# A four-block cross-attention kernel: in the last block all copies of transposed weights go to ScalarE, and half of the next step's exponentials are issued behind them

## The chip, the cores and the metric

The kernel runs on one core of a Trainium2 chip. The time is device time in microseconds (us) of one execution; the median of several runs counts. The engines of the core are TensorE (PE in the profile; PEld is its weight load), VectorE (DVE), ScalarE (ACT), GpSimd (POOL) and SyncE (SP, which issues most DMAs here).

## What is computed

Four blocks follow one another on `x` of shape (8, 112, 256), with a context of shape (8, 375, 192). Blocks 0 and 1 are self attention, cross attention and a gated MLP; block 2 is one cross attention; all of these have 16 heads of width 64. The last block has 16 heads of width 16, and is the one in which the change lies:

```python
h = _layernorm(x, ln1_w, ln1_b)
qkv = (h @ qkv_w + qkv_b).reshape(B, T, 3, H, HD)
q, k, v = [qkv[:, :, i].transpose(0, 2, 1, 3) for i in range(3)]
attn = jnp.einsum('bhtd,bhsd->bhts', q, k) * scale
attn = jnp.where(causal[None, None], neg, attn)
attn = jnp.where(tgt_mask[:, None, None, :], neg, attn)
attn = jax.nn.softmax(attn, axis=-1)
sa = jnp.einsum('bhts,bhsd->bhtd', attn, v).transpose(0, 2, 1, 3).reshape(B, T, C)
x = x + sa @ proj_w + proj_b
h = _layernorm(x, ln2_w, ln2_b)
...
attn = jnp.einsum('bhtd,bhsd->bhts', q, k) * scale
attn = jnp.where(enc_mask[:, None, None, :], neg, attn)
attn = jax.nn.softmax(attn, axis=-1)
ca = jnp.einsum('bhts,bhsd->bhtd', attn, v).transpose(0, 2, 1, 3).reshape(B, T, C)
x = x + ca @ out_w + out_b
h = _layernorm(x, ln3_w, ln3_b)
h = jax.nn.gelu(h @ mlp1_w + mlp1_b, approximate=False)
x = x + h @ mlp2_w + mlp2_b
```

Here q, k and v of the second attention come from `h` and the context. All is fp32.

## The kernel before, in words

**Stages and steps.** The work is cut into stages 0 to 9: stages 0 to 2 and 3 to 5 are blocks 0 and 1, stage 6 is block 2, stage 7 the causal self attention of the last block, stage 8 its cross attention, stage 9 its MLP. An attention stage is a list of steps. A step takes some heads of one batch: in stage 8 four heads against 375 context positions (four steps a batch, 32 in all), in stage 7 eight heads against 112 positions (two steps a batch, 16 in all). The causal steps of a batch stand among the steps of stage 6 or 8, as soon as their batch is ready. From the last step of stage 6 on, all steps have 16-wide heads; this stretch is called "the block" below.

**One step** (`add_step`) has three parts. `emit_s` makes the scores by matmuls (L943) into two PSUM tiles of the "s" pool, which has just two, and calls `softmax` for each block of heads. For 16-wide heads `softmax` issues, head by head, a DVE operation (L894) that subtracts the scores from the mask, writes the result to SBUF and gives its minimum, and an exponential on ACT (L898) with that minimum as bias, which also sums the row into `bsums`. For 64-wide heads it issues one DVE maximum (L905), exponentials (L911), a reciprocal (L917) and a POOL multiplication (L920). `emit_t` transposes the weights on PE (L962), one PSUM tile of the "mm" pool for each bank of 4 x 112 columns (three banks in a cross step, two in a causal step), and copies the tile to SBUF (`wT`) by `evac`. `emit_pv` multiplies with the values (L985) and evacuates the result to `oT`.

**The "mm" ring** has four PSUM tiles. All of PE's products but the scores take their tile from it, in turn; a product waits until the tile of four allocations ago has been copied away.

**`evac`** copies from PSUM to SBUF on ACT (L343, L345, L347) or DVE (L351, L353, L355). It keeps a running load for both, to which `busy` adds the work that isn't `evac`'s, and takes the engine that would be done first by this account.

**Order.** PE's order is written out by a planner (`Plan`). In the main loop, iteration i emits the scores of step i + 2, on odd i the PV parts of steps i - 1 and i, then the transposes of step i + 1, and between these fillers that are due: projections (L663, L685, L710), keys (L751 and L760), values (L826 and L835), output products (L629), normalized `x` transposed (L597, evacuated to `hT`), MLP products (L1233). An item states what it depends on, and after how many us of planned time it may follow. The other engines' queues are set by a scheduler at build time, except for what stands in `tc.keep_in_program_order`. Each engine works its queue in order.

**Normalization of 16-wide heads** comes once for each batch, after its last step: item ("R", st, b) takes the reciprocal of the sums on DVE (L1019) and has POOL broadcast it to `rb` (L1020), and item ("N", st, b) transposes `rb` on PE (L1026) and scales `oT` on DVE (L1028). "R" may follow 4.0 us of planned time after the scores of the batch's last step. An output product (L629, added to `x` at L633) then prepares the next normalization (DVE L566, L568, L570; POOL L572, L574, L576).

Of the kernel before, what the change touches and what calls it, by code (L numbers as in the profile page):

```python
# [11 lines left out]
AF = mybir.ActivationFunctionType  # L12
# [3 lines left out]
B, T, D = 8, 112, 256  # L16
S, DC = 375, 192
# [282 lines left out]
def kernel(ctx: ExitStack, tc: tile.TileContext, a: dict, out: bass.AP):  # L300
    nc = tc.nc
# [19 lines left out]
    plan = Plan(RINGS, ARENA, lambda k: 512 if k[0] == "v" else S if k[0] == "k" and k[1] in (1, 4, 6, 8) else 4 * T)  # L321
# [7 lines left out]
    SEG = [0, 0, 0, 1, 1, 1, 2, 2, 2, 2]  # L329
    load = {"act": 0.0, "dve": 0.0}  # L330

    def busy(eng, us):
        load[eng] = max(load[eng], plan.now) + us
# [537 lines left out]
    bsums, pairs = {}, {}  # L871

    def add_step(st, b, blocks, dh, nk, qs, ks, qap, kap, vtile, mask, opos, ochunk, last=False, pair=None):
# [3 lines left out]
        s = len(steps)  # L877
        nch = (nk + P - 1) // P
        dp = 64 if dh == 64 else 32
        heads = [h for blk in blocks for h in blk]  # L880
        cell = {}

        def softmax(blk, ps):
            ns = len(blk) // 2
            sv = ps[:, :, : ns * nk].rearrange("p b (s k) -> p b s k", k=nk)
            pr = ppool.tile([T, 2, ns, nk], F32, tag="pr", name="pr")
            nm = small.tile([T, 2, 4], F32, tag="nm", name="nm")
            if dh == 16:

                for n, h in enumerate(blk):
                    bk, sl = n % 2, n // 2
                    nc.vector.tensor_tensor_reduce(  # L894
                        pr[:, bk, sl, :], sv[:, bk, sl, :], mask(), -1.0, -0.01 * NEG, ALU.add, ALU.min,
                        nm[:, bk, sl : sl + 1],
                    )
                    nc.scalar.activation(  # L898
                        pr[:, bk, sl, :], pr[:, bk, sl, :], AF.Exp, bias=nm[:, bk, sl : sl + 1], scale=-1.0,
                        accum_out=bsums[(st, b)][:, h : h + 1],  # L900
                    )
                    busy("dve", 0.16 + 0.00104 * nk)
                    busy("act", 0.46 + 0.00084 * nk)
                return pr
            nc.vector.tensor_reduce(nm[:, :, :ns], sv, AX.X, ALU.max, negate=True)  # L905
            busy("dve", 0.16 + 0.00104 * 2 * ns * nk)
            sums = small.tile([T, 2, 4], F32, tag="sums", name="sums")
            rinv = small.tile([T, 2, 4], F32, tag="rinv", name="rinv")
            for n in range(len(blk)):
                bk, sl = n % 2, n // 2  # L910
                nc.scalar.activation(  # L911
                    pr[:, bk, sl, :], sv[:, bk, sl, :], AF.Exp, bias=nm[:, bk, sl : sl + 1],
                    accum_out=sums[:, bk, sl : sl + 1],
                )
                busy("act", 0.46 + 0.00084 * nk)
                if nch > 1:
                    nc.vector.reciprocal(rinv[:, bk, sl : sl + 1], sums[:, bk, sl : sl + 1])  # L917

                    tc.keep_in_program_order(
                        nc.gpsimd.tensor_scalar_mul(pr[:, bk, sl, :], pr[:, bk, sl, :], rinv[:, bk, sl : sl + 1])  # L920
                    )
                    busy("dve", 0.16)
            if nch == 1:
                nc.vector.reciprocal(rinv[:, :, :ns], sums[:, :, :ns])  # L924
                tc.keep_in_program_order(
                    nc.gpsimd.tensor_tensor(  # L926
                        pr, pr, rinv[:, :, :ns].unsqueeze(3).to_broadcast([T, 2, ns, nk]), ALU.mult
                    )
                )
                busy("dve", 0.16)  # L930
            return pr

        def emit_s():
            if dh == 16 and (st, b) not in bsums:
                bsums[(st, b)] = small.tile([T, H], F32, tag="bsums", name="bsums")
            tiles = [ps_s.tile([T, 2, 512], F32, tag="s", name="s") for _ in blocks]

            order = [(i, n) for i, blk in enumerate(blocks) for n in range(len(blk))]
            if dh == 16:
                order.sort(key=lambda e: (e[1] // 2, e[0]))  # L940
            for i, n in order:
                h = blocks[i][n]
                nc.tensor.matmul(  # L943
                    tiles[i][:, n % 2, (n // 2) * nk : (n // 2 + 1) * nk], lhsT=qap(h), rhs=kap(h),
                    start=True, stop=True,
                )
            for i, blk in enumerate(blocks):
                pr = softmax(blk, tiles[i])
                for n, h in enumerate(blk):
                    cell[h] = pr[:, n % 2, n // 2, :]  # L950


        if nch == 1:
# [4 lines left out]
        def emit_t(bank):  # L958
            pt = mm_tile()
            kl = min(P, nk - bank[0][1] * P)  # L960
            for i, (h, c) in enumerate(bank):
                nc.tensor.transpose(  # L962
                    pt[:kl, i * T : (i + 1) * T], cell[h][:, c * P : c * P + kl], ident[:T, :T]
                )
            wt = tpool.tile([P, 448], F32, tag="wT", name="wT")
            n = len(bank) * T
            evac(wt[:kl, :n], pt[:kl, :n], n)
            for i, (h, c) in enumerate(bank):
                cell[(h, c)] = wt[:kl, i * T : (i + 1) * T]

        def emit_pv():
# [18 lines left out]
            if pair is not None and not second:  # L990
# [11 lines left out]
        par = P // dp  # L1002
        plan.add(Item(("S", s), len(heads) / par * nk * 4 / 2400 + 0.19, emit_s, uses=uq + uk,
                      deps=[] if mask is None else [(("mask", b if nk == S else "self"), 3.0)]), False)
        for i, bank in enumerate(banks):
            plan.add(
                Item(("T", s, i), 0.1 * len(bank), lambda bank=bank: emit_t(bank), deps=[(("S", s), 0)]), False
            )
        plan.add(
            Item(("PV", s), 0.193 * nch * len(heads) / par + 0.25, emit_pv, uses=uv,  # L1010
                 deps=[(("T", s, i), 0) for i in range(len(banks))]), False
        )
        steps.append(len(banks))
        if last:

            def emit_norm():

                rs = small.tile([T, H], F32, tag="rsum", name="rsum")
                nc.vector.reciprocal(rs, bsums.pop((st, b)))  # L1019
                nc.gpsimd.tensor_copy(rb, rs.unsqueeze(2).to_broadcast([T, H, 16]))  # L1020

            def emit_scale():
                rf = rb.rearrange("p h d -> p (h d)")
                ps = mm_tile()
                for c in range(2):
                    nc.tensor.transpose(ps[:, c * T : (c + 1) * T], rf[:, c * P : (c + 1) * P], ident[:T, :T])  # L1026
                cols = slice(b * T, (b + 1) * T)
                nc.vector.tensor_tensor(  # L1028
                    oT[:, 0:2, cols], ps[:, : 2 * T].rearrange("p (c t) -> p c t", t=T), oT[:, 0:2, cols], ALU.mult
                )  # L1030
                busy("dve", 0.31)

            prev = [(k, 0) for k in norms[-1:]]
            norms.append(("N", st, b))
            plan.add(Item(("R", st, b), 0, emit_norm, s + 0.4, deps=[(("S", s), 4.0)] + prev, seg=SEG[st]))
            plan.add(
                Item(("N", st, b), 0.2, emit_scale, s + 0.9, deps=[(("R", st, b), 2.0), (("PV", s), 1.2)], seg=SEG[st])
            )
# [65 lines left out]
    def first_of(st, b):  # L1104
        return at[(st, b, 0)]
# [183 lines left out]
    st = 0  # L1289
# [79 lines left out]
    for seg in range(3):  # L1369
        lo, hi = cuts[seg], cuts[seg + 1]  # L1370

        for s in (lo, lo + 1):
            for k in plan.items[("S", s)].uses + plan.items[("PV", s)].uses:
                mk = plan.maker.get(k)
                if mk is None or plan.items[mk].done:
                    continue
                if plan.items[mk].begin is not None:
                    plan.require(mk)
                else:
                    plan.drain(mk)  # L1380
        for i in range(lo - 2, hi):
            plan.step = i
            left = plan.pace(i, seg)
            plan.close_jobs()
            if lo <= i + 2 < hi:
                plan.main(("S", i + 2))

            if lo <= i < hi and (i - lo) % 2 == 1:
                plan.main(("PV", i - 1))
                plan.main(("PV", i))  # L1390
            if lo <= i + 1 < hi:
                n = steps[i + 1]
                share = left / (n + 2)
                left -= plan.fill(2 * share)
                for k in range(n):
                    plan.main(("T", i + 1, k))
                    left -= plan.fill(min(left, share))
            plan.fill(left)
            plan.open_jobs(1 if i + 1 >= first_of(8, 0) else 2, i + 3.5, seg)
    plan.step = len(steps)  # L1400
# [37 lines left out]
```

## Time and profile before

| | |
|---|---|
| median of 3 runs | 1664.54 us (1663.47 to 1664.8) |
| the profiled execution | 1663.88 us, span 1662.1 us |
| PE busy in the span | 1632.3 us (98%) |
| DVE busy | 825.7 us (50%) |
| ACT busy | 769.4 us (46%) |
| POOL busy | 718.3 us (43%) |
| DMA | 39.51 MB, mean 24 GB/s |
| exponentials of 16-wide heads (L898), 256 | 124.7 us busy, mean 488 ns, and 50.1 us of ACT idle before them until DVE's L894 |
| copies to `wT` on ACT (L347), 289 | 151.1 us, mean 533 ns |
| copies to `wT` on DVE (L355), 191 | 115.0 us, mean 612 ns |

The span is the time from the first to the last instruction on the core; the run's time is a little more. A group's row in the profile gives busy time, mean duration, and the idle time of that engine just before the group with what ended it. In the order of time, durations of neighbouring instructions on one engine overlap a little; the distance from start to start is what an instruction costs in a full queue. A view of waits gives, for a waiting line and what released it, the total, the number of times, and the longest.

### The profile page before, as it was taken

To read this page: it belongs to the slowest core of one execution; us is meant where nothing else is said; L and a number is where in the kernel's file an instruction comes from. 1 tells how busy PE (TensorE), PEld (TensorE's weight loads), DVE (VectorE), ACT (ScalarE), POOL (GpSimd) and SP (SyncE) were. 2 spreads that over 40 slices of the span, in tenths; PEclk is the share of its full clock that TensorE was granted. 3 is DMA by queue.
4 is the path that set the end of the run, shared out by engine and by line. 5 is a ranking of instruction groups with operands and counts; after the bars stand their busy time and mean duration, and the time that the engine had idled before them with its cause. 6 is when DMAs were issued, how large, how long until landed. Compare 5 with 4: busy or idle time off the path is not lost.

```text
span 1662.1 us, 30117 instructions
## 1 busy us (share of the span) xinstructions
PE 1632.3 (98%) x11772; PEld 1141.7 (69%) x11772; DVE 825.7 (50%) x2193; ACT 769.4 (46%) x2420; POOL 718.3 (43%) x689
## 2 busy tenths in 40 slices
PE   9999999999999999999999999999999999998999
PEld 7777666666667878666666665666666666765568
DVE  3444454544532344545444552344455556787762
ACT  3554434444531445434444452234444555676662
POOL 1324455556632223355565570364564448322110
DMA  5012020000101011000000010100000000000000
GB/s 186 5 50 56 3 87 1 1 26 1 52 29 45 1 29 52 26 1 30 1 2 26 1 45 29 33 23 1 1 1 1 16 1 26 30 2 2 2 2 23
DMA packets 26566, 39.51 MB, mean 24 GB/s; under 512 B 1543, under 2 KB 21559, under 8 KB 26423
## 3 DMA queue, kind: packets, MB, share of 16 engines
q1 hardware_dynamic: 25495, 36.74, 7.0%
q8 instruction: 93, 1.52, 0.4%
q10 hardware_dynamic: 864, 0.79, 0.1%
q14 instruction: 50, 0.41, 0.1%
q0 software_dynamic: 64, 0.05, 0.0%
HBM read 35.88 MB, written 0.92 MB: 22 GB/s over the span
## 4 chain that ended last, share of the span: by engine, by line
PE 91%; DVE 4%; ACT 3%; issue 1%; POOL 1%; DMA 0%; ACTq 0%; POOLq 0%; DVEq 0%
PE mm L629 12%; PE mm L663 11%; PE s L943 10%; PE mm L985 10%; PE mm L962 9%; PE mm L751 8%; PE mm L785 7%; PE mm L1198 6%; PE mm L760 5%; PE mm L794 4%; PE mm L710 4%; PE mm L1233 2%; ACT pr L898 2%; DVE pr L894 1%; ACT pr L911 1%
## 5 line engine op out<-in xcount | busy, mean ns | idle before, releaser
L920 POOL TENSOR_SCALAR pr<-pr,rinv 112x375 f32<-112x375 f32 x384 | 467.7, 1235 | 338.3 <-DVE rinv L917 338.1
L911 ACT ACTIVATE pr<-s,nm 112x375 f32<-112x375 f32 (+1 forms) x640 | 303.0, 491 | 168.4 <-DVE nm L905 166.2
L355 DVE COPY arena<-mm 128x375 f32<-128x375 f32 (+4 forms) x187 | 111.8, 608 | 296.8 <-PE mm L760 139.0
L962 PEld LDWEIGHTS mm<-ident,pr 112*128 112x128 f32 (+2 forms) x1920 | 208.7, 151 | 49.0 <-issue 20.7
L905 DVE TENSOR_REDUCE nm<-s 112x2 f32<-112x750 f32 (+1 forms) x224 | 206.3, 957 | 69.3 <-PE s L943 65.8
L962 PE MATMUL mm<-ident,pr 112*128 112x112 f32 (+2 forms) x1920 | 233.0, 263 | 6.9 <-POOL pr L920 1.5
L347 ACT COPY arena<-mm 128x375 f32<-128x375 f32 (+4 forms) x181 | 94.1, 520 | 300.6 <-PE mm L760 142.0
L347 ACT COPY wT<-mm 128x448 f32<-128x448 f32 (+2 forms) x289 | 151.1, 533 | 130.7 <-PE mm L962 130.7
L943 PE MATMUL s<-arena 64*112 64x375 f32 (+3 forms) x1792 | 211.2, 394 | 0.1
L985 PEld LDWEIGHTS mm<-wT,arena 128*64 128x64 f32 (+5 forms) x3840 | 160.0, 129 | 38.2 <-issue 20.8
L985 PE MATMUL mm<-wT,arena 128*64 128x112 f32 (+5 forms) x3840 | 180.5, 261 | 0.3 <-ACT wT L347 0.2
L943 PEld LDWEIGHTS s<-arena 64*112 64x112 f32 (+1 forms) x1792 | 113.8, 172 | 79.5 <-issue 30.0
L898 ACT ACTIVATE pr<-pr,nm 112x112 f32<-112x112 f32 (+1 forms) x256 | 124.7, 488 | 50.1 <-DVE nm L894 50.1
L926 POOL TENSOR_TENSOR pr<-pr,rinv 112x896 f32<-112x896 f32 x32 | 53.8, 1683 | 210.1 <-DVE rinv L924 199.2
L911 ACT ACTIVATION_READ_ACCUMULATOR pr<-s,nm 112x1 f32 x640 | 134.4, 210 | 0.0
L355 DVE COPY wT<-mm 128x448 f32<-128x448 f32 (+2 forms) x191 | 115.0, 612 | 18.1 <-PE mm L962 17.5
L572 POOL TENSOR_TENSOR rs<-ve,mhalf 128x1 f32<-128x1 f32 x70 | 39.3, 564 | 192.1 <-DVE ve L570 191.9
L917 DVE RECIPROCAL rinv<-sums 112x1 f32<-112x1 f32 x384 | 62.1, 162 | 90.1 <-ACT pr L911 89.5
L785 PE MATMUL mm<-L_xattn_Wv,ctxA 128*128 128x512 f32 (+1 forms) x192 | 92.2, 600 | 1.4 <-DVE wT L355 1.0
L751 PE MATMUL mm<-ctxA,L_xattn_Wk 128*128 128x375 f32 x256 | 91.6, 482 | 0.0
L633 DVE TENSOR_TENSOR x<-mm,x 128x256 f32<-128x256 f32 x70 | 29.6, 423 | 113.3 <-PE mm L629 113.2
L663 PE MATMUL mm<-hT,L_xattn_Wq 128*128 128x224 f32 x384 | 83.4, 361 | 0.1
(131 smaller groups left out, 2224.3 us busy)
## 6 DMA issues: line engine op xcount, KB each, us to landing
L_xattn_Wo<-in_L_xattn_Wo_dram SPq DMA_DIRECT2D x3, 1024.0 KB, 16.8
L_xattn_w_ff<-in_L_xattn_w_ff_dram SPq DMA_DIRECT2D x3, 1024.0 KB, 5.2
L_xattn_Wv<-in_L_xattn_Wv_dram SPq DMA_DIRECT2D x4, 512.0 KB, 5.5
L_xattn_Wq<-in_L_xattn_Wq_dram SPq DMA_DIRECT2D x2, 1024.0 KB, 4.6
L_xattn_Wp<-in_L_xattn_Wp_dram SPq DMA_DIRECT2D x2, 1024.0 KB, 5.7
L_xattn_wq<-in_L_xattn_wq_dram SPq DMA_DIRECT2D x2, 1024.0 KB, 4.7
L_xattn_wo<-in_L_xattn_wo_dram SPq DMA_DIRECT2D x2, 1024.0 KB, 5.5
L_xattn_mlp_w<-in_L_xattn_mlp_w_dram SPq DMA_DIRECT2D x2, 1024.0 KB, 5.1
```

The lines of the kernel that those rows point to most:

```text
L347: nc.scalar.copy(dst, src)
L355: nc.vector.tensor_copy(dst, src)
L629: nc.tensor.matmul(ps[:, :D], lhsT=oT[:, c, t * P : (t + 1) * P], rhs=got[wv or w][:, c, :], start=(c == 0), stop=(c == n - 1),)
L663: nc.tensor.matmul(ps[:, i * 2 * T : (i + 1) * 2 * T], lhsT=got[w][:, k, m * P : (m + 1) * P], rhs=hT[:, k, lo:hi], start=(k == 0), stop=( ...
L751: nc.tensor.matmul(ps[:, :S], lhsT=got[wv][:, (2 * u + i) * P : (2 * u + i + 1) * P], rhs=ctxA[:, cols], start=True, stop=False,)
L785: nc.tensor.matmul(ps[: KCH[c][1], :], lhsT=lhs(ctxA, slice(0, KA), c), rhs=got[w][:, hf * 512 : (hf + 1) * 512], start=True, stop=False,)
L905: nc.vector.tensor_reduce(nm[:, :, :ns], sv, AX.X, ALU.max, negate=True)
L911: nc.scalar.activation(pr[:, bk, sl, :], sv[:, bk, sl, :], AF.Exp, bias=nm[:, bk, sl : sl + 1], accum_out=sums[:, bk, sl : sl + 1],)
L920: nc.gpsimd.tensor_scalar_mul(pr[:, bk, sl, :], pr[:, bk, sl, :], rinv[:, bk, sl : sl + 1])
L943: nc.tensor.matmul(tiles[i][:, n % 2, (n // 2) * nk : (n // 2 + 1) * nk], lhsT=qap(h), rhs=kap(h), start=True, stop=True,)
L962: nc.tensor.transpose(pt[:kl, i * T : (i + 1) * T], cell[h][:, c * P : c * P + kl], ident[:T, :T])
L985: nc.tensor.matmul(po[p0 : p0 + dp, blk * T : (blk + 1) * T], lhsT=got[vk][:kl, hv * dp : (hv + 1) * dp], rhs=wt, start=(c == 0 and par(h) ...
```

## The change

For 16-wide heads (`dh == 16`), `softmax` no longer issues the exponentials, but appends them to a list `late`. `emit_s` issues the first half of the list after the step's DVE operations. A new item ("E", s) issues the other half, in program order; the main loop emits it for step i + 2 after the transposes of step i + 1. The transposes of a step depend on its "E" item, and so does "R", which may now follow 2.0 us after "E". The copies of 16-wide heads' transposed weights are always ACT's. The account of `busy` has smaller constants for the exponentials (0.28 in place of 0.46 us) and the DVE operations (0.08 in place of 0.16).

```diff
         heads = [h for blk in blocks for h in blk]
-        cell = {}
+        cell, late = {}, []
...
-                    nc.scalar.activation(
-                        pr[:, bk, sl, :], pr[:, bk, sl, :], AF.Exp, bias=nm[:, bk, sl : sl + 1], scale=-1.0,
-                        accum_out=bsums[(st, b)][:, h : h + 1],
-                    )
-                    busy("dve", 0.16 + 0.00104 * nk)
-                    busy("act", 0.46 + 0.00084 * nk)
+                    busy("dve", 0.08 + 0.00104 * nk)
+
+                    def exp(pr=pr[:, bk, sl, :], nm=nm[:, bk, sl : sl + 1], h=h):
+                        busy("act", 0.28 + 0.00084 * nk)
+                        return nc.scalar.activation(
+                            pr, pr, AF.Exp, bias=nm, scale=-1.0, accum_out=bsums[(st, b)][:, h : h + 1]
+                        )
+
+                    late.append(exp)
                 return pr
...
                 pr = softmax(blk, tiles[i])
                 for n, h in enumerate(blk):
                     cell[h] = pr[:, n % 2, n // 2, :]
+            for _ in range(len(late) // 2):
+                late.pop(0)()
+
+        def emit_late():
+
+            for exp in late:
+                tc.keep_in_program_order(exp())
...
-            evac(wt[:kl, :n], pt[:kl, :n], n)
+            if dh == 16:
+                nc.scalar.copy(wt[:kl, :n], pt[:kl, :n])
+                busy("act", 0.04 + 0.00084 * n)
+            else:
+                evac(wt[:kl, :n], pt[:kl, :n], n)
...
+        if dh == 16:
+            plan.add(Item(("E", s), 0, emit_late, deps=[(("S", s), 0)]), False)
         for i, bank in enumerate(banks):
             plan.add(
-                Item(("T", s, i), 0.1 * len(bank), lambda bank=bank: emit_t(bank), deps=[(("S", s), 0)]), False
+                Item(("T", s, i), 0.1 * len(bank), lambda bank=bank: emit_t(bank),
+                     deps=[(("E" if dh == 16 else "S", s), 0)]), False
             )
...
-            plan.add(Item(("R", st, b), 0, emit_norm, s + 0.4, deps=[(("S", s), 4.0)] + prev, seg=SEG[st]))
+            plan.add(Item(("R", st, b), 0, emit_norm, s + 0.4, deps=[(("E", s), 2.0)] + prev, seg=SEG[st]))
...
                     plan.main(("T", i + 1, k))
                     left -= plan.fill(min(left, share))
+            if ("E", i + 2) in plan.items and lo <= i + 2 < hi:
+                plan.main(("E", i + 2))
             plan.fill(left)
```

## The prediction

> **What bounds the kernel now.** I read the page first (TensorE, PE, is busy 98% of the span, and 91% of the chain of waits is PE: this is a TensorE kernel), then the busy time by stretch, to find where PE is not full.
>
> ```profile
> core 0: us, PE busy (x) PEld busy (x) DVE busy (x) ACT busy (x) POOL busy (x), PEclk, DMA share, GB/s
> 1150.00:1200.00 50.00, 50.00 (x366) 34.66 (x363) 25.02 (x55) 22.61 (x61) 24.81 (x22) 1.00 0.00 1
> ...
> 1500.00:1525.00 25.00, 20.52 (x233) 14.39 (x231) 19.88 (x85) 17.39 (x66) 4.45 (x9) 1.00 0.00 1
> 1525.00:1550.00 25.00, 21.97 (x224) 14.64 (x224) 17.50 (x58) 15.97 (x47) 3.72 (x7) 1.00 0.01 2
> ...
> 1575.00:1600.00 25.00, 25.00 (x213) 14.16 (x214) 15.69 (x50) 13.68 (x39) 3.14 (x5) 1.00 0.01 2
> ```
>
> Columns: stretch, length, then busy time of each engine. At 1150 PE has no gap. Between 1500 and 1550 it has 7.5 us of gaps in 50, and DVE and ACT are 70 to 80% busy. The eight windows from 1430 to 1620, the block of 16-wide heads alone, hold 190 us with 175.5 of PE: 14.5 us idle. That is all the change can win, give or take pauses that the modelled ends hide. At 1575 to 1600 PE is full again, with the MLP products (L1233).
>
> The waits of PE in 1430 to 1620 say what ends the gaps:
>
> ```profile
> PE mm L751 <- DVE wT L355: 2.4, 2, 1.4
> PE mm L826 <- DVE wT L355: 1.4, 2, 0.9
> PE mm L751 <- ACT wT L347: 1.3, 2, 0.8
> PE mm L826 <- DVE arena L351: 1.3, 1, 1.3
> PE mm L962 <- ACT hT L343: 1.1, 1, 1.1
> ```
>
> (total us, times, longest.) PE does not lack data for its own step: the filler products (L751, L826) lack a PSUM buffer, for the "mm" ring has four and the three banks of transposed weights hold three of them until they are copied. One step in order of time shows why the copies are late (PE, then DVE, then ACT):
>
> ```profile
> 1521.33 0.90 PE L943 MATMUL s<-arena 32*112 32x375 f32 x8
> 1522.16 1.41 PE L962 MATMUL mm<-ident,pr 112*128 112x112 f32 x12
> 1523.40 0.61 PE L826 MATMUL mm<-ctx_w,ctxA 128*128 128x256 f32 x2
> 1524.92 0.70 PE L826 MATMUL mm<-ctx_w,ctxA 128*128 128x256 f32 x2 [0.91 <-DVE wT L355]
> ...
> 1522.37 0.55 DVE L894 CUSTOM_DVE_ANT_0 pr<-s,cm 112x375 f32<-112x375 f32 x1 [0.69 <-PE s L943]
> ...
> 1524.25 1.15 DVE L355 COPY wT<-mm 128x448 f32<-128x448 f32 x2
> ...
> 1521.10 1.37 ACT L347 COPY wT<-mm 128x448 f32<-128x448 f32 x3
> 1522.96 0.61 ACT L898 ACTIVATE pr<-pr,nm 112x375 f32<-112x375 f32 x1 [0.49 <-DVE nm L894]
> 1523.57 0.60 ACT L898 ACTIVATE pr<-pr,nm 112x375 f32<-112x375 f32 x1
> ...
> 1525.35 0.51 ACT L347 COPY wT<-mm 119x448 f32<-119x448 f32 x1
> ```
>
> The transposes (L962) of the step before are done at 1523.5. Their copies stand behind the next step's work: on DVE behind four mask reductions (L894, one each 0.47), on ACT behind four exponentials (start to start 0.60). So the first copy starts at 1524.25 and PE waits.
>
> **What the change moves** (instructions counted in the built queues of both kernels).
>
> 1. All copies of transposed weights of 16-wide steps go to ACT: 71 more on ACT, 71 fewer on DVE, 57 of them in the block. On ACT one takes 0.42 start to start ((1.37 - 0.53) / 2 above), on DVE 0.53. In return the balancer sends DVE nine more key and query evacuations and ACT 23 of hT and oT. Summing the block's queues by start-to-start times from its rows (0.60 and 0.37 per exponential of 375 and 112, 0.42 per copy, 0.47 and 0.20 per reduction, 0.2 to 0.6 for the rest): ACT 133 to 159 us, DVE 148 to 118. ACT becomes the fuller engine: 159 of some 185, 86%. Nothing issues a DMA differently, SP's queue is the same.
>
> 2. Half of a step's exponentials (two of four, or four of eight) are issued behind the copies of the step before. A copy now waits for two reductions and two exponentials after the scores: 0.2 + 0.55 + 1.2 = 1.95 us after them, against 2.1 (DVE) to 3.2 (ACT) now; the third copy is done at 1.95 + 1.26 = 3.2 against 3.2 to 3.6. The price: the second pair ends at 3.2 + 1.2 = 4.4 us after the scores instead of 3.2, and the next step's transposes, the first bank of which takes heads of both halves, wait for it. Queued behind the waiting first pair on ACT are the three copies, and PE's filler waits for those.
>
> 3. The reciprocal of the sums (L1019) is planned from the second half and stands later on DVE, mostly behind two of the next step's reductions. Its waits for ACT are 9.9 us in ten times in the block, and behind one of them (1530.41) stood the hT evacuation for which PE lost the 1.1 us above. Three of POOL's broadcasts (L1020) fall behind a normalization (L572, L574, L576: 0.56 + 1.23 + 0.73 = 2.5 us) and three transposes of them (L1026) stand one to four places later on PE. POOL is busy only 43 of 190 us here. Cost of each between 0 and 2.5; I take 0, since PE meets L1026 several us after the reciprocal.
>
> **The sum, by replaying steps with these durations.** In the step above the second pair of the previous step now ends at 1521.8 + 1.2 = 1523.0, so the transposes end at 1524.1 (0.7 later), with L1026 now among them 1524.3. The copies start after the first pair at 1524.2. The first filler needs the first bank's buffer: 1524.6. Two L826 tiles (1.2) and L835 (0.63) give the next scores at 1526.45, against 1526.18: 0.3 lost. In the next step PE waited 1.1 for hT; now hT follows the first pair at 1529.15 and is done by 1530.05, when the transposes are due: next scores at 1533.25 against 1533.78, so 0.8 won. Going on so, scores come 0.8 earlier at 1538.79, 1.4 at 1545.03 and 2.1 at 1563.92. That is 2.1 us in 8 steps; the steps from 1496.96 to 1521.33, with two of the causal kind, give 0.9 in 5. So 3.0 in 13 steps, 0.23 a step. The 29 steps from 1430.94 to 1575.48 give 6.7 us. The 7 steps after them, most with MLP products: 0, PE is full; if that cover were gone they would win the same 0.23 each. The end of the block: the last group of xn transposes (L597) now stands behind the last PV, so its evacuation (0.47 + 0.1) is bare: +0.6. A replay by hand leaves hand-offs out: some 0.03 us a step, +1.0. The stage of 64-wide heads before 1430, where the causal steps stand between steps of 7 to 10 us and PE is over 95% busy: 0, between -1 and +2 (PE idles 4.2 us between 1350 and 1450). Sum -6.7 + 0.6 + 1.0 = -5.1.
>
> The profiled execution ran 1663.88 with a span of 1662.1; the median of three is 1664.54, 2.4 over that span. 1662.1 - 5.1 + 2.4 = 1659.4 us.
>
> The Trainium skill's page "TensorEngine Tiling (Array Packing)", section "PSUM Bottleneck", speaks against the change: when array tiling makes TensorE faster, copying out of PSUM can become the limit, and both ScalarE and VectorE should be used for it. By that rule three copies in a row on ACT, 1.26, replace two on DVE beside one on ACT, 1.06: 0.2 us in each of 32 cross steps, 6.4 us lost, 1671. The row at 1524.25 shows the copy held by its place in the queue and not by the copying, so the sum above goes by the row.
>
> **The rivals.**
>
> *No change (1664.5).* What the copies win, the second pair gives back, as in the step at 1521.33. For it: that step. Against: of the 13 replayed steps most with filler win, and DVE's stall at L1019 goes in any case.
>
> *ACT becomes the bound (slower).* A cross step costs ACT 4 x 0.60 + 3 x 0.42 = 3.66, and 0.3 for its share of other evacuations: 4.0 us. Thirteen steps now take less, score to score: 2.66, 3.43, 3.31, 3.55, 3.46, 2.01, 3.90, 2.80, 3.46, 3.65, 3.93, 3.65, 3.04. If none can borrow from a neighbour and the long steps win nothing, these stretch by 9.1 us: 1673.6. It decides from the point where the second pair reaches the transposes late in short steps too, ACT over 90% busy in the windows from 1450 to 1575. For it: ACT already waits 41 us in the block for reductions (L898 behind L894), time that it can't always use. Against: short steps stand beside long ones (2.01 before 5.47), and a pair then has 7.5 for ACT's 8.
>
> *More than replayed.* The named waits of PE in the block (on wT, arena, hT, oT and x) are 13.1 us; if all go, 1664.5 - 13.1 = 1651.4. For it: DVE, the fuller engine now, loses a fifth of its work. Against: ACT at 86% will leave some.
>
> That the queue is not as written is no rival: the built ACT queue of the changed kernel has two exponentials, three copies, two exponentials in all cross steps, but for evacuations between.
>
> **How the numbers follow.** Chances: forecast 0.46, more 0.10, no change 0.22, ACT the bound 0.22. About 0.2%, 3.3 us, is what a measurement tells from no change; so faster 0.56, same 0.22, slower 0.22. The forecast's own range is 1656 to 1661. The whole range goes down to the third rival, 1651.4, and half way into the second, 1669; beyond lie some 2 in 10.
>
> **What would show it.** Right: waits of L751 and L826 for wT below 3 us together (6.1 now); the reciprocal's wait for ACT below 4; ACT at 155 to 160 busy and DVE near 115 in the block; waits of L962 for exponentials (L902 in the changed file) up from 0.3, but below 6; scores of the last step some 5 us earlier. Wrong: L962's waits for exponentials larger than what left L751 and L826, the short steps at 4 us, or a difference that arises before 1430.

## The result and the profile after

The changed kernel took 1667.49 us (median of 13 runs, 1665.53 to 1670.84), the kernel before 1664.8 in 13 runs beside it (1663.4 to 1666.19). The ratio is 1.0019, with a 95% interval of 1.0011 to 1.0028. The change cost about 0.2%; the forecast was a gain of 0.3%.

Two distances in the order of time tell where it went: from the first scores of the last block's cross attention (at 1428.28 before) to the last scores (called the block's length here), and from the last scores to the end of TensorE's last product (the tail). Both are read in the one profiled execution of each kernel.

| | before | after | difference |
|---|---|---|---|
| profiled execution, span | 1662.1 | 1667.9 | +5.8 |
| first scores of the block, since a step at 1236 | 192.64 | 193.09 | +0.45 |
| block's length | 186.14 | 182.88 | -3.26 |
| tail | 44.51 | 52.48 | +7.97 |

The block became shorter, as intended; the tail lost more than twice as much. (The three differences are +5.2; the other 0.7 of the spans arose before 1236, where the change has nothing.) The profiled execution of the changed kernel was 2.2 above its median and that of the kernel before 0.9 below, so the medians differ by 2.7 only; the last section says what is known of this scatter.

In the block the profile after looks as it should. The busy time by stretch, for the windows shown of before:

```profile
core 0: us, PE busy (x) PEld busy (x) DVE busy (x) ACT busy (x) POOL busy (x), PEclk, DMA share, GB/s
...
1500.00:1525.00 25.00, 22.98 (x256) 15.99 (x248) 16.46 (x80) 22.80 (x80) 4.44 (x9) 1.00 0.01 3
1525.00:1550.00 25.00, 23.80 (x268) 15.86 (x272) 16.10 (x57) 18.33 (x54) 5.85 (x10) 1.00 0.00 1
1575.00:1600.00 25.00, 25.00 (x211) 14.66 (x209) 8.87 (x34) 17.09 (x47) 3.14 (x5) 1.00 0.00 1
```

TensorE's gaps in 1500 to 1550 fell from 7.5 us to 3.2, and ACT is the fuller engine now. The waits of PE in 1430 to 1620 (total, times, longest):

```profile
PE mm L972 <- ACT pr L902: 4.9, 15, 1.1
PE mm L826 <- ACT wT L978: 1.2, 3, 0.6
PE mm L751 <- ACT wT L978: 1.1, 2, 0.6
PE mm L629 <- ACT wT L978: 1.0, 2, 0.5
```

The fillers' waits for a PSUM buffer (L751, L826) fell from 6.1 us on `wT` and 2.2 on `arena` to 2.3. In their place the transposes (L972, L962 before) wait for the late exponentials, 4.9 us in 15 times: small ones, but for one of 1.1, which lies in the last step. The step that the prediction showed, in order of time, now starts at 1520.27 (start, duration, engine, line, operation, count; in brackets the idle time before it and what ended it):

```profile
1520.27 0.90 PE L946 MATMUL s<-arena 32*112 32x375 f32 x8
...
1520.86 0.61 ACT L902 ACTIVATE pr<-pr,nm 112x375 f32<-112x375 f32 x1
...
1522.21 0.32 PE L972 MATMUL mm<-ident,pr 112*128 112x112 f32 x1 [0.28 <-ACT pr L902]
...
1523.24 1.38 ACT L978 COPY wT<-mm 128x448 f32<-128x448 f32 x3
...
1523.81 1.13 PE L826 MATMUL mm<-ctx_w,ctxA 128*128 128x256 f32 x4 [0.29 <-ACT wT L978]
1524.50 0.62 ACT L902 ACTIVATE pr<-pr,nm 112x375 f32<-112x375 f32 x1
...
1524.87 0.70 PE L835 MATMUL mm<-ctx_w,ctxB 64*128 64x256 f32 x4
```

The transposes wait 0.28 for the previous step's late pair, the filler waits 0.29 in place of 0.91, and the late pair follows the copies. That is the order as foretold. The copies start no earlier here than before (2.97 after the scores, against 2.92), and this step by itself loses 0.4, from its scores to the next (4.85 before, 5.23 now; 0.3 was foretold). The step after it wins 1.3 (7.60 to 6.26).

The tail is where the time went. First the kernel before, from its order of time:

```profile
1618.44 0.56 PE L962 MATMUL mm<-ident,pr 112*128 112x112 f32 x3 [0.32 <-DVE oT L355]
...
1619.27 0.32 PE L962 MATMUL mm<-ident,pr 112*128 112x112 f32 x1 [0.28 <-ACT pr L898]
...
1620.04 1.02 PE L962 MATMUL mm<-ident,pr 112*128 112x112 f32 x8 [0.45 <-DVE wT L355]
...
1620.89 0.60 PE L597 MATMUL mm<-ident,xn 128*128 128x128 f32 x4
...
1621.42 1.36 PE L985 MATMUL mm<-wT,arena 128*32 128x112 f32 x48
1621.53 0.99 DVE L351 TENSOR_SCALAR hT<-mm,vcols 128x256 f32<-128x256 f32 x2 [0.23 <-PE mm L597]
1621.70 1.28 ACT L1260 ACT_TABLE_LOAD   x1
...
1622.72 7.17 PE L1233 MATMUL mm<-hT,L_xattn_mlp_w 128*128 128x256 f32 x32
```

The transposed `xn` (L597) are evacuated by DVE, both halves in 0.99, under the last PV parts; ACT loads its table for Gelu at the same time, and the MLP products follow without a gap. The changed kernel, same view:

```profile
1617.53 0.32 PE L972 MATMUL mm<-ident,pr 112*128 112x112 f32 x1 [1.14 <-ACT pr L902]
...
1618.12 1.99 PE L972 MATMUL mm<-ident,pr 112*128 112x112 f32 x9 [0.27 <-ACT pr L902]
...
1620.04 2.08 PE L999 MATMUL mm<-wT,arena 128*32 128x112 f32 x48
...
1620.75 1.28 ACT L1277 ACT_TABLE_LOAD   x1
1622.04 3.71 ACT L1277 ACTIVATE oT<-oT 128x2048 f32<-128x2048 f32 x2
...
1622.05 0.66 PE L597 MATMUL mm<-ident,xn 128*128 128x128 f32 x4
...
1623.34 0.70 PE L1250 MATMUL mm<-hT,L_xattn_mlp_w 128*128 128x256 f32 x2 [0.64 <-DVE hT L351]
1625.66 0.55 ACT L343 ACTIVATE hT<-mm,vcols 128x256 f32<-128x256 f32 x1
...
1626.26 9.47 PE L1250 MATMUL mm<-hT,L_xattn_mlp_w 128*128 128x256 f32 x30 [2.21 <-ACT hT L343]
```

Three things are new. TensorE waits 1.14 for a late exponential, with nothing to fill (in the kernel before, its waits in this last step were 0.32, 0.28 and 0.45). The balancer has given one half of `hT` to ACT (L343), where it stands behind the table load and two Gelus until 1626.2; TensorE waits 2.21 for it. And TensorE is slow: 9 transposes take 1.99 (8 took 1.02 before), PV 2.08 in place of 1.36, 30 products 9.47 where 32 took 7.17 (these are counts of records; each fp32 product of the MLP has two). The windows name the reason, in the column PEclk:

```profile
1610.00:1615.00 5.00, 4.52 (x74) 3.25 (x73) 3.24 (x14) 3.91 (x14) 1.06 (x2) 1.00 0.02 5
1615.00:1620.00 5.00, 3.40 (x21) 2.70 (x18) 1.12 (x6) 4.13 (x12) 1.84 (x3) 0.82 0.01 2
1620.00:1625.00 5.00, 3.40 (x55) 2.56 (x54) 0.82 (x2) 4.77 (x4) 0.00 (x0) 0.84 0.00 0
1625.00:1630.00 5.00, 3.74 (x9) 2.99 (x10) 0.97 (x2) 1.20 (x2) 0.00 (x0) 0.50 0.00 0
1630.00:1635.00 5.00, 5.00 (x21) 4.23 (x20) 2.03 (x5) 1.06 (x1) 0.00 (x0) 0.82 0.00 0
```

The granted clock was halved twice: for (0.18 + 0.16) x 2 x 5 = 3.4 us in 1615 to 1625, and for 5 + 1.8 = 6.8 us in 1625 to 1635. In the same windows of before it is 1.00.

### The profile page after: what moved, and what is told of

It reads as the page before. It is cut to its first block, busy times and chain, and to the rows that moved or that the text cites. A ratio compares the mean times of both kernels' runs of the same rounds, so it can differ in the third digit from the quotient of the medians.

```text
span 1667.9 us, 30145 instructions
## 1 busy us (share of the span) xinstructions
PE 1638.9 (98%) x11772; PEld 1146.0 (69%) x11772; DVE 784.4 (47%) x2108; ACT 801.2 (48%) x2505; POOL 718.1 (43%) x689
## 4 chain that ended last, share of the span: by engine, by line
PE 90%; ACT 4%; DVE 3%; POOL 2%; issue 1%; DMA 0%; ACTq 0%; POOLq 0%; DVEq 0%
PE mm L629 12%; PE mm L663 11%; PE mm L999 10%; PE s L946 10%; PE mm L972 9%; PE mm L751 8%; PE mm L785 7%; PE mm L1215 6%; PE mm L760 5%; PE mm L794 4%; PE mm L710 4%; ACT pr L902 2%; PE mm L1250 2%; POOL pr L923 1%; PE mm L597 1%
## 5 line engine op out<-in xcount | busy, mean ns | idle before, releaser
L923 POOL TENSOR_SCALAR pr<-pr,rinv 112x375 f32<-112x375 f32 x384 | 467.7, 1236 | 333.7 <-DVE rinv L920 333.6
L972 PEld LDWEIGHTS mm<-ident,pr 112*128 112x128 f32 (+2 forms) x1920 | 210.1, 151 | 54.7 <-issue 20.7
L972 PE MATMUL mm<-ident,pr 112*128 112x112 f32 (+2 forms) x1920 | 237.2, 264 | 10.3 <-ACT pr L902 4.9
L347 ACT COPY wT<-mm 128x448 f32<-128x448 f32 (+2 forms) x232 | 122.2, 534 | 122.9 <-PE mm L972 122.8
L751 PE MATMUL mm<-ctxA,L_xattn_Wk 128*128 128x375 f32 x256 | 91.5, 481 | 0.0
L355 DVE COPY wT<-mm 128x448 f32<-128x448 f32 (+2 forms) x120 | 73.6, 614 | 16.8 <-PE mm L972 16.3
```

The costliest lines, as they stand in the source:

```text
L347: nc.scalar.copy(dst, src)
L355: nc.vector.tensor_copy(dst, src)
L751: nc.tensor.matmul(ps[:, :S], lhsT=got[wv][:, (2 * u + i) * P : (2 * u + i + 1) * P], rhs=ctxA[:, cols], start=True, stop=False,)
L972: nc.tensor.transpose(pt[:kl, i * T : (i + 1) * T], cell[h][:, c * P : c * P + kl], ident[:T, :T])
```

## The experiments

All times are medians; the ratio is to the kernel before, run beside it. Block and tail are of one profiled execution each. The block of the changed kernel repeats at 182.88 in e1, e2 and e3, which leave it as it is, and that of the kernel before lies between 185.96 and 186.37 in the profiles of before, e4 and e10. Where an edit adds lines, line numbers shift by a few (L974 or L964 for L972, L1252 for L1250, and so on).

| kernel | us | ratio, 95% | block | tail |
|---|---|---|---|---|
| before | 1664.8 | | 186.14 | 44.51 |
| changed | 1667.5 | 1.0019 (1.0011 to 1.0028) | 182.88 | 52.48 |
| e1 hT on DVE | 1662.6 | 0.9989 (0.998 to 0.9998) | 182.88 | 47.07 |
| e2 hT early | 1663.6 | 0.999 (0.9981 to 0.9999) | 182.88 | 44.82 |
| e3 products in the pause | 1666.8 | 1.0012 (1.0003 to 1.0021) | 182.88 | 48.90 |
| e4 before, hT behind Gelu | 1671.1 | 1.004 (1.0027 to 1.0053) | 185.96 | 50.01 |
| e5 copies alone | 1672.2 | 1.0041 (1.0029 to 1.0054) | 192.84 | 44.97 |
| e6 late exponentials alone | 1659.7 | 0.9966 (0.9954 to 0.9979) | 180.06 | 45.42 |
| e7 changed, end mended | 1660.6 | 0.9974 (0.9963 to 0.9984) | 182.95 | 43.94 |
| e8 e7, third copy on DVE | 1659.3 | 0.9961 (0.9949 to 0.9974) | 180.95 | 43.94 |
| e9 late alone, end mended | 1658.3 | 0.9961 (0.9948 to 0.9975) | 180.08 | 43.93 |
| e10 constants alone | 1665.1 | 1.0006 (0.9997 to 1.0014) | 186.37 | 44.11 |
| e11 three of four late | 1662.5 | 0.9986 (0.9977 to 0.9995) | 183.50 | 44.28 |

**e1: both halves of the evacuation on DVE.** In `add_norm_transposes`, against the changed kernel:

```diff
-                    evac(
-                        hT[:, c, ts[0] * P : ts[0] * P + n], ps[:, c * n : (c + 1) * n], n,
-                        scale=col(g, c), bias=col(bt, c),
-                    )
+                    dst, src = hT[:, c, ts[0] * P : ts[0] * P + n], ps[:, c * n : (c + 1) * n]
+                    if (st, gi) == (9, 2):
+                        nc.vector.tensor_scalar(dst, src, col(g, c), col(bt, c), ALU.mult, ALU.add)
+                        busy("dve", 0.157 + 0.00104 * n)
+                    else:
+                        evac(dst, src, n, scale=col(g, c), bias=col(bt, c))
```

> The changed kernel (1667.5), but both halves of the evacuation of the next to last group of transposed xn go to DVE; everything before it is untouched, and TensorE's order is the same. Theory 1 (the loss is in the tail: one half stood on ACT behind the table load and two Gelus until 1626.2, and TensorE's granted clock was halved after that pause): the second half is done one DVE operation after the first, 0.5 us, so the MLP products go on at 1623.8 instead of 1626.3, -2.5; with no pause above 1.2 us the clock stays at 1.00 there and the 32 products take 7.2 instead of 10.2, another -2.5 or so: 1662 to 1663, without the clock's part 1665. Theory 2 (ACT's load and the late exponentials in the block are the price, and another wait follows at once): 1666.5 to 1668.5.

Measured 1662.55, block 182.88, tail 47.07: 5.4 of the tail's 8.0 came back, and the block did not move. The clock did not stay at 1.00: it was halved for 3.4 us from 1616.5, behind the wait of 1.14 for the late exponential that e1 leaves in place, which costs 1.4 of this tail (9 transposes 2.00 in place of 1.12 and PV 1.85 in place of 1.36, the durations that e3 has at full clock). Behind that, in its order of time the 32 products take 7.19 after a pause of 0.64, the evacuation that was foretold to be bare:

```profile
1620.67 0.66 PE L597 MATMUL mm<-ident,xn 128*128 128x128 f32 x4
1621.96 7.19 PE L1252 MATMUL mm<-hT,L_xattn_mlp_w 128*128 128x256 f32 x32 [0.64 <-DVE hT L603]
```

The larger part of the loss sat in the tail, in that half evacuation; ACT's load in the block is not what made the kernel slower.

**e2: the group of transposes before the last PV parts.** One line in `emit_pv` of the changed kernel, and nothing said of an engine:

```diff
         def emit_pv():
+            if s == 174:
+                plan.require(("hT", 9, 2))
             second = pair in pairs
```

> The changed kernel (1667.5), but the same group of transposes (L597) stands before the last two PV parts, as in the kernel before, by one line in the planning; with that the balancer puts both halves of its evacuation on DVE by itself. Theory 1 (the place of this group, through the balancer, is the whole of the loss in the tail but for the late exponentials): the MLP products begin right after PV, some 1.0 earlier than in the kernel with both halves on DVE alone: 1661 to 1662.3, with the clock at half only in 1618 to 1621.6 or not at all. Theory 2 (late exponentials and ACT's load are the price): 1666.5 to 1668.5.

The balancer indeed chose DVE for both halves; the tail is 44.82, 7.7 shorter than the changed kernel's and within 0.3 of the kernel before. The time, 1663.59, missed the foretold 1661 to 1662.3. A reason lies ahead of the edit's place. In this profiled execution the stretch from 1236 to the block took 194.7 in place of 193.1, with a halved clock in one window:

```profile
1360.00:1380.00 20.00, 18.43 (x117) 9.86 (x115) 11.68 (x28) 11.34 (x37) 14.25 (x13) 0.91 0.00 1
```

e4, which has nothing of the change, shows the same 0.91 there, and the profiles of before and of the changed kernel show 1.00. Executions of either kernel differ by this: the three of e2's eleven runs whose clock averaged 1.000 took 1660.9 to 1661.4. So the intervals of e1 and e2 overlap, and the tails of the profiles tell the two apart better than the medians.

**e3: products in the pause.** The wait for ACT stays, but TensorE has something to do:

```diff
+                if (st, gi) == (9, 2):
+                    warm(14)
```

> The changed kernel (1667.5), with 14 products of the identity with itself (128x128, 0.15 us each at full clock) after the same group of transposes, so that TensorE works through most of its pause; the wait for ACT's half stays. Their result is not used. Theory 1a (the half clock after 1625 is an answer to the pause): the wait for ACT stays (until about 1626.2), but the clock is 1.00 after it, the 30 products take 6.8 instead of 9.5: 1664.5 to 1665.3. Theory 1b (these products are slow from something else, such as the Gelu on ACT beside them): they still take 0.31 each, 1667 to 1668.

```profile
1622.52 3.29 PE L376 MATMUL mm<-ident 128*128 128x128 f32 x28
1625.64 0.60 PE L1252 MATMUL mm<-hT,L_xattn_mlp_w 128*128 128x256 f32 x2
1626.97 6.74 PE L1252 MATMUL mm<-hT,L_xattn_mlp_w 128*128 128x256 f32 x30 [0.72 <-ACT hT L343]
```

```profile
core 0: us, PE busy (x) PEld busy (x) DVE busy (x) ACT busy (x) POOL busy (x), PEclk, DMA share, GB/s
...
1625.00:1630.00 5.00, 4.28 (x24) 3.54 (x23) 1.45 (x3) 1.91 (x2) 0.00 (x0) 1.00 0.02 3
```

(The 28 records of L376 are the 14 added products.) TensorE still goes on only when ACT's half has come, but the 30 records then take 6.74 in place of 9.47, with Gelu beside them as ever and the clock at 1.00. So the slow products were slow by the clock, and it stayed up where the pause was filled. The tail is 48.90: in these two profiles 4.4 of the 8.0 lost are waits and 3.6 the clock, of which 0.9 is the first half clock, ahead of the added products, which this execution does not have. The median came down by 0.7 only, less than the 2.2 to 3.0 foretold. This profile has a half clock at 1360, and the two of eleven runs whose clock averaged 1.000 took 1664.6 and 1665.5; where the other runs lost their clock is not known. By the medians, then, filling the pause was worth less than the 2.7 that the profile shows for it.

**e4: the kernel before, with one half of the same evacuation behind Gelu.**

```diff
+                if (st, gi) == (9, 2):
+                    plan.require(("gelu", 9, 0))
                 ps = mm_tile()
...
+                    if (st, gi, c) == (9, 2, 1):
+                        tc.keep_in_program_order(
+                            nc.scalar.activation(dst, src, AF.Identity, bias=col(bt, c), scale=col(g, c))
+                        )
...
```

> The kernel before (1664.8), with nothing of the change, but one half of the same evacuation on ACT, behind the table load and the first two Gelus. Theory 1: TensorE waits at the MLP products from 1623.1 until the Gelus (1626.7) and the half (0.5) are done, 1627.3: +4.2; if its clock then halves for 6.8 us as in the changed kernel, another +2.5 to +3: 1669 to 1672. Theory 2 (the wait has room behind it, the end is set elsewhere): at most +1, 1665.8.

```profile
1624.68 3.71 ACT L1266 ACTIVATE oT<-oT 128x2048 f32<-128x2048 f32 x2
...
1628.29 0.55 ACT L606 ACTIVATE hT<-mm,vcols 128x256 f32<-128x256 f32 x1
...
1628.89 3.44 PE L1239 MATMUL mm<-hT,L_xattn_mlp_w 128*128 128x256 f32 x8 [3.79 <-ACT hT L606]
```

1671.06, 6.3 above the kernel before: nothing of the change is in this kernel, and this one place costs more than the whole change did. TensorE waits 3.79 for the half on ACT, and its clock is halved for 3.4 us behind the wait (0.84 in 1625 to 1630, 0.82 in 1630 to 1635). The tail is 5.5 longer than in the kernel before; the rest of this profile's time is the half clock at 1360. With e1, the cause is shown from both sides.

**e5 and e6: each half of the change alone**, both with e1's edit, so that the tail does not disturb. e5 issues all exponentials before the copies:

```diff
-            for _ in range(len(late) // 2):
+            for _ in range(len(late)):
                 late.pop(0)()
```

> One half of the change: all copies of transposed weights on ACT, but all exponentials of a step issued before them (the accounts' constants as in the changed kernel, and both halves of the last but one hT evacuation on DVE, as in the first of these runs, 1662.6). To be read by the block, from the first scores of 16-wide heads to the last: 186.1 before, 182.9 changed. Theory 1 (what counts is that a copy stands behind two exponentials in place of four): the copies start 0.2 + 0.55 + 4 x 0.6 = 3.15 after the scores, later than before on either engine (2.1 on DVE), so the block is no shorter than before: 186 to 190, time 1665 to 1670. Theory 2 (what counts is that DVE is relieved of 57 copies): most of the gain stays, 183 to 184.5, time 1662 to 1664.

e6 leaves the copies to the balancer:

```diff
-            if dh == 16:
-                nc.scalar.copy(wt[:kl, :n], pt[:kl, :n])
-                busy("act", 0.04 + 0.00084 * n)
-            else:
-                evac(wt[:kl, :n], pt[:kl, :n], n)
+            evac(wt[:kl, :n], pt[:kl, :n], n)
```

> The other half: half of the exponentials behind the copies of the step before, and the copies given to ACT or DVE by the balancer (constants and hT as in the run beside it). The block: 186.1 before, 182.9 changed. Theory 1: ACT's copies start at 1.95 after the scores as in the changed kernel, DVE's still behind four reductions at 2.1 and beside them, so most of the gain stays or more: 181.5 to 184.5, time 1661 to 1664. Theory 2 (DVE's relief counts): near before, 185 to 187, time 1664.5 to 1667.

The block of e5 is 192.84, 6.7 longer than before (a half clock in 1475 to 1500 has up to 1.7 of it), and more than foretold. Its waits of PE in the block:

```profile
PE mm L828 <- ACT wT L980: 5.6, 7, 1.8
PE mm L753 <- ACT wT L980: 4.6, 6, 1.2
```

The block of e6 is 180.06, better than foretold: 6.1 shorter than before and 2.8 shorter than with the whole change. Its largest waits:

```profile
PE mm L974 <- ACT pr L904: 2.4, 8, 0.6
PE mm L753 <- ACT wT L347: 1.1, 2, 0.6
PE mm L828 <- ACT wT L347: 0.6, 2, 0.3
```

So the late exponentials bring all of the gain, and the other half, all copies on ACT, takes 2.8 of it back. (The later place of the reciprocal is in both e5 and e6; no run takes it apart from the late exponentials.) The effects do not simply add up: copies on ACT cost 6.7 behind all exponentials (less by up to the 1.7 of clock) and 2.8 behind half of them. Of the 111 copies to `wT` from the block's start on, ACT makes 57 before, 111 in the changed kernel, and 67 in e6. Theory 2, the relief of DVE, has fallen.

**e10: is e6's gain the balancer's?** e6 and the changed kernel have other constants in the account too. e10 is the kernel before with these (and e1's edit, which keeps there what is there):

```diff
-                    busy("dve", 0.16 + 0.00104 * nk)
-                    busy("act", 0.46 + 0.00084 * nk)
+                    busy("dve", 0.08 + 0.00104 * nk)
+                    busy("act", 0.28 + 0.00084 * nk)
```

> The kernel before with nothing but the new constants of the account (0.28 for the exponentials, 0.08 for the mask operations) and the last but one hT evacuation on DVE, as it is there anyway. It tells how much of the late exponentials' gain (block 186.1 to 180.1) is the balancer's other choice, for that run had these constants too. Theory 1 (the order on ACT's queue is what counts): block 185 to 187.5, time 1664 to 1666. Theory 2 (the balancer had misjudged the load): block 180 to 183.5, time 1659.5 to 1662.5.

The block is 186.37, 0.2 longer than before. The constants are not it: ACT makes 66 of the 111 copies here, about as many as in e6.

**e7: the end mended.** The changed kernel with e1's and e2's edits, and in `emit_s`:

```diff
-            for _ in range(len(late) // 2):
+            for _ in range(len(late) if s == 175 else len(late) // 2):
                 late.pop(0)()
```

> The changed kernel with its end mended: the last but one group of xn transposes before the last PV parts and its evacuation on DVE (as in the second run, tail from the last scores to TensorE's end 44.8 there, 1663.6), and the last step alone issues all its exponentials at once. Theory 1 (the late exponentials are bare in the last step, for TensorE waits 1.1 for them with nothing to fill): the transposes end some 1 us earlier after the last scores, and without that pause the clock is not halved there: tail 43.5 to 44.2, time 1660.5 to 1662.5. Theory 2 (a wait for the copies of the step before takes its place, since they now stand behind four exponentials): tail 44.6 to 45.5, time 1663 to 1664.5. The block should stay at 182.9 in both.

1660.56; the tail is 43.94, 0.9 shorter than e2's, and the granted clock averaged over an execution rounds to 1.000 in 7 of 8 runs. The bare wait for late exponentials in the last step was worth about 1 us. What it cost by the clock is not shown: e2's profile has its half clock at 1360, ahead of this edit, and why e7's runs so rarely have one there is open. With the end mended, the change as designed brings 0.26%.

**e8: the third copy on DVE**, on e7:

```diff
+                if nch == 3 and bank[0][1] == 2:
+                    nc.vector.tensor_copy(wt[:kl, :n], pt[:kl, :n])
+                    busy("dve", 0.04 + 0.00104 * n)
+                else:
+                    nc.scalar.copy(wt[:kl, :n], pt[:kl, :n])
+                    busy("act", 0.04 + 0.00084 * n)
```

> The kernel of the run beside it, but the third copy of a cross step (119 x 448) goes to DVE, so that ACT has two copies a step. Theory 1 (ACT, 86% busy in the block, is now the engine that sets the copies' time): the third copy is done at 2.65 after the scores beside ACT's second at 2.8, in place of 3.2, and the late exponentials end 0.4 earlier: block 180.5 to 182.3, time 1658.5 to 1661. Theory 2 (on DVE a copy stands behind four reductions again, and TensorE's filler waits for it as before the change): block 183 to 185.5, time 1662 to 1665.

Block 180.95, 2.0 less than e7, time 1659.3. A copy on DVE, though behind four reductions, is better than a third on ACT.

**e9: late exponentials alone and the mended end**, that is e6 with the edits of e2 and e7.

> The late exponentials alone (copies by the balancer, block 180.1 from first to last scores, tail 45.4, 1659.7), with the mended end (group of xn transposes before the last PV, its evacuation on DVE, all exponentials of the last step at once; tail 43.9 with the copies on ACT). Theory 1 (block and end are independent): block 180.1, tail 43.9, together 3.0 + 3.6 us less than the changed kernel's block and the first run's tail: 1657.3 to 1658.7, the fastest of all. Theory 2 (the balancer shifts other work and gives one part back): 1659 to 1660.5.

Block 180.08, tail 43.93, time 1658.33: the parts add up. It has the lowest median, 6.5 below the kernel before and 9 below the changed one; e8 can't be told from it by its interval.

**e11: three of four exponentials late**, on e9 (`len(late) // 4` in place of `len(late) // 2`).

> The first kernel of this call, with three of four exponentials (six of eight) behind the copies in place of two. Theory 1 (what a copy stands behind is what counts, the second group still arrives in time): a copy on ACT waits for one exponential, 1.35 after the scores: block 178 to 180, 1655.5 to 1658. Theory 2 (the next transposes wait for late exponentials, as they already do for 2.4 us in all): copies are early but three exponentials behind them end 0.6 later against the next transposes in short steps: block 180.5 to 183, 1658.5 to 1661.

```profile
PE mm L974 <- ACT pr L904: 5.4, 18, 0.7
PE mm L828 <- ACT wT L347: 0.4, 2, 0.2
```

The block is 183.50 and the time 1662.5, both even beyond what theory 2 foretold. The fillers hardly wait any more (0.4), but the transposes wait 5.4 us in 18 times for the exponentials. Half is the better share here.

## Why the prediction was wrong

The sign was wrong: foretold -5.1 us, measured +2.7. The step that failed is the term for the end of the block, "its evacuation (0.47 + 0.1) is bare: +0.6". The tail lost 8.0 in the profiled execution. By the runs this is 0.9 for the place of the group behind the last PV (e1's tail less its 1.4 of half clock, against e2's), which is what the term priced; 3.2 for the wait for ACT's half (e3's tail, against e1's in the same way); 0.3 for the late pair of the last step (e2 against before); and 3.6 for the clock. Three things were not in that term:

- *Which engine gets the second half, and what stands before it there.* I priced one DVE half. The built queue of the changed kernel has the other half on ACT behind two Gelus; I had counted how many evacuations change engines, but did not look where each one lands. The account of `evac` can't see it either: the Gelu items add nothing to it with `busy`, so ACT looks free while 1.28 + 3.71 us stand in its queue. It cost 3.2, and e4 has the same stall, longer, without the change.
- *The clock.* A pause of TensorE was priced at its length. Here the clock was also halved behind it, another 3.6 in the profiled execution (the changed kernel against e3), though the medians of these two differ by only 0.7.
- *The last step has no filler.* The second pair's delay was weighed in the middle of the block, where 0.3 is lost; in the last step it is bare (1.14 and 0.27 of waits; undoing it there brings 0.9, e7 against e2). The kernel before waited 1.05 in that step too, so against it the loss is 0.3.

The other steps, by their own numbers:

- *What bounds the kernel*: right. With the wait for buffers gone, the block became shorter.
- *The replayed steps*: close. From the step at 1521.33 on, 0.8, 1.4 and 2.1 us were foretold by 1538.79, 1545.03 and 1563.92; measured 1.0, 1.4 and 2.0. The five steps up to 1521.33 won 2.2 in place of 0.9.
- *0.23 a step for all 29*: mis-sized. The 14 steps up to 1496.96 won nothing (3.2 by that rate), where TensorE was idle for only 2.3 us of 50 in the windows 1450 to 1500 of before; by 1575.48 the gain was 4.75 in place of 6.7, or of some 5.8 with the hand-offs taken off. The rate was taken where the gaps were.
- *The last 7 steps 0*: 0.25 won up to the last but one, 1.75 lost in the step before the last scores, where the planner put the transposes of `rb` and an output product, which now waits 0.48 for a copy. So the block won 3.3 where the sum, without its term for the end, had 5.7.
- *Moving the copies to ACT has no price of its own*: wrong by 2.8 us (e6 against e1), about the 2.4 that the block fell short of the sum. Where the 2.8 arise is shown in part: in 1430 to 1612 the transposes wait 3.5 for the late pair with three copies ahead of it (e7) and 2.4 in e6, and fillers and output products (L753, L828, L631) wait 3.3 and 2.2 for copies. The Trainium skill's page "TensorEngine Tiling (Array Packing)", section "PSUM Bottleneck", says to use both ScalarE and VectorE for copying out of PSUM. The prediction set it aside; e6 and e8 say it was right here in its direction, at 2.8 and 2.0 us and not the 6.4 that I had made of it.
- *Rivals*: ACT did not become the bound: it passed 90% in one of the five windows from 1450 to 1575 (22.80 of 25 in the window at 1500), and most short steps kept their length (2.66 stayed 2.66, 2.01 became 2.11; but 3.55 became 3.98, and the last, 3.05, became 4.79). "No change" names nearly the size of the result, but its mechanism was not it.
- *What would show it*: waits of L751 and L826 for `wT` 2.3 (below 3), the reciprocal's wait for ACT 3.5 (below 4), ACT 157 and DVE 117 busy in 1430 to 1620, L972's waits 4.9 (below 6). These held; the last scores 5 us earlier did not, 3.3 within the block. Of the signs of being wrong, L972's 4.9 stay below what left L751 and L826 in all (9.3 to 2.5), though not below what left their waits for `wT` (3.8). No sign on the list stood behind the last scores, and there the loss was.

## What to carry to other kernels

Where a balancer chooses engines, an edit in one place moves choices in others: compare what each queue holds behind the edit, above all next to long operations that the account leaves out, and price a copy by what stands before it. Treat the last step of a pipeline apart, since nothing fills there what the steps before hide. And try the halves of a change singly: here one brought 6.1 us and the other took 2.8 of them back.

## What was not expected of the hardware

A short pause of TensorE can cost about twice its length: in the changed kernel the waits of 0.64 and 2.21 at 1623 to 1626 were followed by 2.7 us lost at the half clock. The half clocks of these profiles last 3.4 us or 6.8, and most follow pauses much shorter than 3.4: in the changed kernel, the 3.4 us ahead of the first one had TensorE busy for 1.8 us; in e1 2.1, at 1360 to 1380 in e2 and e4 1.9. (e4's second follows a wait of 3.79.) Most stretches of the same grid with 2.0 to 2.5 busy did not halve it (by the records of TensorE's products, whose ends are modelled). The Trainium skill's page "TensorE: Matmul & The Clock Gate", in its part on the HAM clock gate, gives a free-running window of 3413 ns, which the 3.4 and 6.8 agree with, and says that the clock falls after an idle window; here a window that was a little over half busy sufficed, and the measurement decides. The first of these windows in the changed kernel holds transposes alone; whether they count for the clock as other products do, no run here separates.

The same pause is punished in one execution and not in the next. At 1360 to 1380 the profile of before has the same 18.43 us of TensorE in its window as e2, and kept its clock. That the half clocks start on a grid can be seen in e1: they begin at 8.86, 1616.54 and 1660.91, which are 471 and 13 steps of 3.413 us apart. The place of this grid differs between executions, but it does not explain everything. In the changed kernel's profile the window from 1372.42 to 1375.84 holds 1.90 us of TensorE and in e3's the one from 1372.33 to 1375.74 holds 1.89, at the same place in the work; the clock stayed at 1.00 behind the first and was halved behind the second. What share of a window decides, and whether it alone decides, stays open.

By the clock averaged over each execution, the 13 runs of the changed kernel had 2.3 half clocks of 3.4 us each (mean 0.9977), and 27 runs of the kernel before 0.9 (0.9991), at up to 1.7 us each. That is of the size of the scatter between runs. The average does not order the runs, though: of these 27, the eight at 1.000 took 1663.2 on average, the thirteen at 0.999 1665.6, and the six at 0.998 1664.8. e7 to e9 rarely show a half clock, though their pause at 1360 is the same as in e2; why is not known.
